# Attention in float32 on one core: groups of six key tiles with two half tiles copied out of PSUM by VectorE, an earlier load of the first queries, and warm-up products spread out

## The chip, the core and the metric

The kernel runs on one core of a Trainium2 chip. The metric is device time in microseconds of one execution. A core has five engines that run side by side and meet at semaphores: TensorE (PE in the profile, its weight loads PEld), VectorE (DVE), ScalarE (ACT), GpSimd (POOL) and SyncE (SP), which here issues most DMAs. Matrix products are written to PSUM[...]; all else lives in SBUF.

## What is computed

The reference is a chain of four layers on an image of 48 channels and 128 x 128 pixels, each with a group normalisation ahead and a residual sum behind it. The change touches layer 0 alone, which is attention over all 16384 pixels:

```
x = x + _L0_conv_ref(_gn(x), qkv_w, dw_w, proj_w, temperature)
...
qkv = jnp.einsum('bchw,oc->bohw', x, qkv_w)
qkv = conv_general_dilated(qkv, dw_w, ..., feature_group_count=3 * c)
q, k, v = jnp.split(qkv, 3, axis=1)
q = _l2norm(q)
k = _l2norm(k)
attn = softmax(einsum('bnc,bmc->bnm', q, k) * temperature)
out = einsum('bnm,bmc->bnc', attn, v)
return einsum('bchw,oc->bohw', out, proj_w)
```

Layers 1 to 3 (sweeps of 1-d convolutions, a patch convolution, a scan) follow and are the same in both kernels.

## The kernel before

**Conv.** `attention` loads the image in four pieces (SP, L139), computes the statistics of the normalisation (L237 and `group_stats`, L72 to L88) and makes queries, keys and values band by band: eight bands of 16 rows, two steps each. The 1x1 and the depthwise convolution are folded into weights `wt`, and the projection is folded into the values' part of them by four transposes and four products at the start (`pt`). Then 12 products that nobody reads (`keep_running`, tile `p`) run on TensorE ahead of the statistics' products (L74, L83). Normalised queries are written to DRAM (`qm`), each as a high and a low part, and are read back per chunk by `moving(c)`, eight DMAs on SP's queue (L174) into a tile `m`. Keys stay in SBUF as three parts (`kh`, `kl` and a joined rest, `x`). After the last band the first queries are loaded; then a branch on the temperature leads to `attend`.

**Attention.** `attend` loops over 32 chunks of 512 queries. The 64 key tiles of a chunk (each has 128 keys of the first half of the image and 128 of the second) go in groups of G = 5: twelve groups of five and one of four. Per tile, `scores` runs three products for each of the two halves on 64 rows of TensorE (the halves side by side) into two PSUM banks `s`, out of a pool of seven; ScalarE turns each half into `e` by an exponential (SBUF, G + 3 = 8 buffers of two halves). After the scores of a group, TensorE adds up the group before it: `sums` multiplies `e` with the values and their column of ones into the eighth bank, `acc`, the two halves in its upper and lower 64 partitions. So TensorE's order is: scores of group g, sums of group g-1, scores of group g+1, and so on.

**End of a chunk.** Its last group is summed behind the scores of group 0 of the next chunk. `Finish` then copies `acc` to `both` (ScalarE). After group 1, `divide` brings the lower half down (`second`, ScalarE), adds the halves (`y`, VectorE, L505), takes the reciprocal (VectorE, L508) and sends it to the other partitions by three DMAs (`recs`). After group 2, `result` multiplies, adds the residual and takes statistics on VectorE (L515 to L517).

**Order.** Products and ScalarE's instructions in these stages keep the order of the source (`InOrder`, whose line is L49 for all of them). VectorE, GpSimd and SP have no such wrapper: the framework's scheduler sets their order, and waits between engines are on tiles and on buffers of pools that are reused.

```
es = [(j, scores(m, j)) for j in range(g * G, min((g + 1) * G, KT))]
...
for i, e in behind:
    sums(acc, i, e)
if c and g == 0:
    finish = Finish(c - 1, acc)
if c and g == 1:
    finish.divide()
if c and g == 2:
    finish.result()
```

Of the kernel before, what the change touches and what calls it, by code (L numbers as in the profile page):

```python
# [19 lines left out]
F32 = mybir.dt.float32  # L20
F16 = mybir.dt.float16
F32R = mybir.dt.float32r
AF = mybir.ActivationFunctionType
# [4 lines left out]
C = 48  # L28
H = W = 128
N = H * W  # L30
CH = 512
# [65 lines left out]
def keep_running(pe, out, lhsT, rhs, n):  # L97

    for _ in range(n):
        pe.matmul(out, lhsT=lhsT, rhs=rhs, start=True, stop=True)  # L100
# [21 lines left out]
def attention(ctx, tc, x1, mp, const, ins):  # L122
# [3 lines left out]
    nc = tc.nc  # L126
    ident, blk = const["ident"], const["blk"]
    NQ = N // CH
    HALF = N // 2
    PART = 2048  # L130

    images = ctx.enter_context(tc.tile_pool(name="l0_x", bufs=1))
    image = []
    for i in range(HALF // PART):
        t = images.tile([128, PART], F32, name=f"x{i}")
        nc.gpsimd.memset(t[32:64], 0.0)
        for half in range(2):
            at = half * HALF + i * PART
# [20 lines left out]
    absT = kv.tile([128, 1], F32, name="absT")  # L159
    nc.vector.tensor_mul(absT, temp, sgn)  # L160

    def moving(c):

        m = mp.tile([128, 2, CH], F32R, name="m")
        high, low = qm[0:C, c * CH : (c + 1) * CH], qm[C:, c * CH : (c + 1) * CH]
        for half in range(2):
            at = 64 * half
            for i, to, x in (
                (0, 0, high),
                (0, C, low[C:]),  # L170
                (1, 0, low[0:32]),
                (1, 32, low[0:32]),
            ):
                nc.sync.dma_start(m[at + to : at + to + x.shape[0], i].bitcast(F32), x)  # L174
        return m
# [19 lines left out]
    with ExitStack() as a:  # L195
        act, pe = InOrder(tc, nc.scalar), InOrder(tc, nc.tensor)
# [4 lines left out]
        ps = a.enter_context(tc.tile_pool(name="l0_aps", bufs=4, space=PSUM))  # L201
# [5 lines left out]
        NB = H // R  # L207
# [4 lines left out]
        w1 = spare[:, 0 : 4 * 192].rearrange("c (t o) -> c t o", t=4)  # L212
        wt = packed_weights(nc, wp, "wt", ins["l0_w"], ins["l0_dw"], 192, w1)

        values = wt[:, :, 128:192]
        turned = spare[0:64, 4 * 192 : 4 * 192 + CH].rearrange("c (t o) -> c t o", t=4)
        pt = ps1.tile([128, 4, 2, 64], F32, name="pt").rearrange("c t n o -> c t (n o)")
        for t in range(4):
            pe.transpose(pt[0:64, t, :], values[:, t, :], ident)
        act.copy(turned, pt[0:64])  # L220
        pt = ps1.tile([128, 4, 2, 64], F32, name="pt")
        for t in range(4):
            pe.matmul(pt[:, t, 0, :], lhsT=turned[:, t, :], rhs=proj, start=True, stop=True)
        act.copy(values, pt[:, :, 0, :])

        K2 = 64 + C

        def piece(i):
            n, at = divmod(i * CH, PART)
            return image[n][:, at : at + CH]  # L230

        for i in range(NQ // 2 - 4):
            idle = ps.tile([128, CH], F32, name="p")
            keep_running(pe, idle, ident[0:K2], piece(i)[0:K2], 1)
        halves = wp.tile([K2, NQ // 2, 6], F32, name="halves")
        for i in range(NQ // 2):
            nc.vector.bn_stats(halves[:, i, :], piece(i)[0:K2])  # L237
        mean, rstd = group_stats(nc, wp, ps2, halves, const["gmat2"], name="pss")
# [154 lines left out]
            return scale, split, get  # L393

        cur = band(0)
        last = None
        for b in range(NB):
            nxt = band(b + 1) if b + 1 < NB else None
            for y in range(0, R, 8):
                p = [ps.tile([128, CH], F32, name="p") for _ in range(2)]  # L400
                pv = ps1.tile([128, CH], F32, name="pv")
                conv(p, pv, cur, y)
                more = take((b * R + y) * W, p, pv)
                if last:
                    last[1](act, last[2])
                last = more
            cur = nxt

    first = moving(0)
    small = nc.values_load(absT[0:1, 0:1].bitcast(mybir.dt.int32))
    bits = int(np.float32(32.0).view(np.int32))
    keys = kh, kl, rest_k
# [20 lines left out]
@with_exitstack  # L435
def attend(ctx, tc, keys, v, moving, m, x1, absT, const, ins, last):

    nc = tc.nc
    act, pe = InOrder(tc, nc.scalar), InOrder(tc, nc.tensor)
    ident, st = const["ident"], const["st"]
    NQ = N // CH
    KT = N // 2 // 128
    G = 5

    ep = ctx.enter_context(tc.tile_pool(name="l0_e", bufs=G + 3))
    sp = ctx.enter_context(tc.tile_pool(name="l0_b", bufs=1))  # L450
    ep2 = ctx.enter_context(tc.tile_pool(name="l0_add", bufs=1))
    ps_s = ctx.enter_context(tc.tile_pool(name="l0_ps", bufs=7, space=PSUM))
    ps_a = ctx.enter_context(tc.tile_pool(name="l0_pa", bufs=1, space=PSUM))


    sides = [slice(0, 64), slice(64, 128)]

    def scores(m, j):
        s = [ps_s.tile([128, CH], F32, name="s") for _ in sides]
        for n in range(3):  # L460
            k, at = key_tile(keys, n, j)
            for half, part in enumerate(sides):
                pe.matmul(
                    s[half],
                    lhsT=k[part, at],
                    rhs=m[part, n // 2],
                    start=(n == 0),
                    stop=(n == 2),
                )
        e = ep.tile([128, 2, CH], F32, name="e")  # L470
        for half in range(2):
            act.activation(e[:, half], s[half], AF.Exp, scale=absT)
        return e

    def sums(acc, j, e):

        for half, to in enumerate(sides):
            pe.matmul(
                acc[to],
                lhsT=v[:, half * KT + j, :],  # L480
                rhs=e[:, half, :],
                start=(j == 0),
                stop=(j == KT - 1),
            )

    def spare(name):

        return sp.tile([128, CH], F32, name=name)

    class Finish:  # L490


        def __init__(self, c, acc):
            self.c = c
            self.cols = slice(c * CH, (c + 1) * CH)
            self.xres = spare("xres")[0:C]
            nc.sync.dma_start(self.xres, ins["x"][:, self.cols])
            self.both = spare("both")
            act.copy(self.both, acc)

        def divide(self):
            second = spare("second")[0:64]
            act.copy(second, self.both[64:128])
            self.y = spare("y")[0:64]
            nc.vector.tensor_add(self.y, self.both[0:64], second)  # L505

            rec = spare("rec")[0:64]
            nc.vector.reciprocal(rec[32:64], self.y[32:64])  # L508
            self.rec = spare("recs")[0:C]
            for i in range(0, C, 64 - C):  # L510
                nc.sync.dma_start(self.rec[i : i + 64 - C], rec[C:64])

        def result(self):
            y = self.y[0:C]
            nc.vector.tensor_mul(y, y, self.rec)  # L515
            nc.vector.tensor_add(y, y, self.xres)
            nc.vector.bn_stats(st[:, self.c, :], y)  # L517
            nc.sync.dma_start(x1[:, self.cols], y)

    def end():  # L520

        cols = slice(N - CH, N)
        xres = spare("xres")[0:C]
        nc.sync.dma_start(xres, ins["x"][:, cols])
        o = spare("both")
        act.copy(o, acc)
        p = ps_s.tile([128, CH], F32, name="s")[0 : 64 + C]
        pe.matmul(p, lhsT=add, rhs=o, start=True, stop=True)
        rec = spare("rec")[0:C]
        nc.vector.reciprocal(rec, p[64 : 64 + C])  # L530
        nc.vector.tensor_mul(rec, p[0:C], rec)
        nc.vector.tensor_add(const["end"], rec, xres)
        nc.vector.bn_stats(st[:, NQ - 1, :], const["end"])

    names = {("f", 0): "xres", ("f", 1): "both", ("hl", 0): "second", ("hl", 1): "y"}
    own = {key: spare(name) for key, name in names.items()}

    def get(name, n):
        return own[name, n]

    scale, split = last
    scale(get)
    add = adder(nc, ep2, ident)
    behind, finish, acc, ahead = [], None, None, m
    for c in range(NQ):
        m = ahead
        for g in range(-(-KT // G)):
            es = [(j, scores(m, j)) for j in range(g * G, min((g + 1) * G, KT))]
            if g == 0 and c + 1 < NQ:
                ahead = moving(c + 1)  # L550
            if c == 0 and g == 2:
                split(act, get)
            for i, e in behind:
                if i == 0:
                    acc = ps_a.tile([128, CH], F32, name="acc")
                sums(acc, i, e)
            if c and g == 0:
                finish = Finish(c - 1, acc)
            if c and g == 1:
                finish.divide()  # L560
            if c and g == 2:
                finish.result()
            behind = es
    for i, e in behind:
        sums(acc, i, e)
    end()
# [1403 lines left out]
```

## Time and profile before

| What | Value |
|---|---|
| median of 3 runs | 7298.08 us (7297.69 to 7302.37) |
| profiled execution | 7313.33 us, span 7311.5 us |
| PE busy | 5935.4 us (81% of the span) |
| ACT busy | 4575.9 us (63%) |
| DVE busy | 3442.6 us (47%) |
| POOL busy | 2869.3 us (39%) |
| exponentials `e<-s` | 4096, mean 694 ns |
| products `acc<-e,v` | 8192 records, two per product, mean 597 ns |
| products `s<-m` | 3 x 4096, mean 389 to 421 ns |
| from the first score product to the last sum | 267.7 to 3677.3 us |

The page divides the span into 40 slices of 183 us; a digit is the busy share in tenths. The first slice and a half are the conv, then attention runs to about the twentieth slice, then come the other layers. An instruction's mean duration is longer than its share of the engine's time where instructions overlap: exponentials follow each other every 0.58 us, and the two halves of a score product run side by side.

### The profile page before, as it was taken

Reading aid. Unit: us, or ns where it says so; the run is one execution under the profiler, and the core shown is the slowest. Engines: PE = TensorE matmul, PEld = TensorE weight load, DVE = VectorE, ACT = ScalarE, POOL = GpSimd, SP = SyncE. Lnnn points to the kernel's source line nnn. Section 1 sums busy time; section 2 is a strip of 40 time slices with the busy share of each in tenths; the row PEclk is TensorE's granted clock in tenths of the full one; section 3 lists DMA queues with packets and bytes.
Section 4 is the critical chain, followed back from the end, with each engine's and each line's share of the span. In section 5 each row is a group of like instructions: output and inputs, shape, how many; then the busy total and the mean of one; then the engine's idle time right before and its main releaser. Section 6 shows DMA issues by size and latency. Waiting matters only on the chain.

```text
span 7311.5 us, 198657 instructions
## 1 busy us (share of the span) xinstructions
PE 5935.4 (81%) x89706; PEld 3563.8 (49%) x89706; DVE 3442.6 (47%) x3012; ACT 4575.9 (63%) x6826; POOL 2869.3 (39%) x655
## 2 busy tenths in 40 slices
PE   8899999999999999999999999455545545555555
PEld 3455555555555555555577755243433434444444
DVE  7400000000000000000044534799999999999998
ACT  3577777777777777777733023666676666666665
POOL 3200000000000000000010322699999999999998
PEclk9999999999999999999999999677767666666666
DMA  4200000000000000000010020565556666666775
GB/s 81 60 7 10 8 7 10 9 6 10 10 8 7 10 9 7 10 10 8 8 31 21 6 51 16 128 165 157 161 155 166 160 156 159 158 164 167 180 179 147
DMA packets 201818, 515.72 MB, mean 71 GB/s; under 512 B 41859, under 2 KB 73650, under 8 KB 199058
## 3 DMA queue, kind: packets, MB, share of 16 engines
q1 hardware_dynamic: 194135, 495.59, 26.4%
q8 instruction: 704, 11.53, 0.7%
q10 hardware_dynamic: 6827, 7.35, 0.4%
q14 instruction: 152, 1.25, 0.1%
HBM read 447.73 MB, written 29.36 MB: 65 GB/s over the span
## 4 chain that ended last, share of the span: by engine, by line
PE 58%; DVE 26%; issue 6%; POOL 4%; ACT 2%; DMA 2%; SPq 1%; ACTq 0%; DVEq 0%; POOLq 0%
PE acc L49 24%; DVE h L1722 22%; PE s L49 21%; PE p L49 7%; POOL h L1715 3%; PE y L49 2%; DMA du<-rep 1%; PE pc L49 1%; DVE xb L49 1%; PE pp L49 1%; PE po L49 1%; DVE rn L360 1%; ACT dA L49 1%; DVE y L49 0%; POOL y L1118 0%
## 5 line engine op out<-in xcount | busy, mean ns | idle before, releaser
L49 ACT ACTIVATE e<-s,absT 128x512 f32<-128x512 f32 x4096 | 2450.5, 694 | 884.2 <-PE s L49 741.7
L1715 POOL TENSOR_TENSOR h<-du,bt 128x3072 f32<-128x3072 f32 (+1 forms) x386 | 2559.2, 6667 | 94.7 <-DMA du<-rep 67.7
L1722 DVE TENSOR_TENSOR_SCAN h<-dA,carry,h 128x1024 f32<-128x1024 f32 x864 | 1940.0, 2325 | 40.6 <-ACT dA L49 27.0
L49 PE MATMUL acc<-e,v 128*64 128x512 f32 x8192 | 1849.4, 597 | 0.0
L49 ACT ACTIVATE dA<-dt,a 128x1024 f32<-128x1024 f32 x1152 | 1287.3, 1118 | 870.4 <-DVE h L1722 859.2
L49 PE MATMUL y<-h,cw 128*32 128x48 f32 x49152 | 900.0, 246 | 945.1 <-issue 503.7
L505 DVE TENSOR_TENSOR y<-both,second 64x512 f32<-64x512 f32 x31 | 21.2, 683 | 3021.6 <-ACT second L49 3021.6
L49 PEld LDWEIGHTS y<-h,cw 128*32 128x32 f32 x49152 | 810.0, 140 | 1073.2 <-issue 664.8
L789 POOL MEMSET xb<- 128x256 f32 (+1 forms) x2 | 0.7, 408 | 3383.3 <-ACT absT L420 3383.3
L49 PEld LDWEIGHTS acc<-e,v 128*64 128x64 f32 x8192 | 551.3, 137 | 1083.4 <-issue 1077.9
L49 PE MATMUL s<-m,kh 64*128 64x512 f32 x4096 | 956.0, 421 | 17.0 <-DMA m<-qm 16.5
L49 PE MATMUL s<-m,x 64*128 64x512 f32 x4096 | 914.6, 390 | 1.2 <-DMA m<-qm 1.1
L49 PE MATMUL s<-m,kl 64*128 64x512 f32 x4096 | 903.8, 389 | 0.0
L49 PEld LDWEIGHTS s<-m,kh 64*128 64x128 f32 x4096 | 473.1, 184 | 467.9 <-ACT e L49 289.6
L1722 DVE TENSOR_TENSOR_SCAN h<-dA,h 128x1024 f32<-128x1024 f32 x288 | 634.9, 2268 | 44.8 <-ACT dA L49 37.0
L49 PEld LDWEIGHTS s<-m,x 64*128 64x128 f32 x4096 | 477.7, 184 | 84.0 <-issue 6.7
L49 PEld LDWEIGHTS s<-m,kl 64*128 64x128 f32 x4096 | 448.1, 185 | 49.4
L49 PE MATMUL yz<-ev,sel 128*8 128x48 f32 x4096 | 192.7, 260 | 272.4 <-ACT ev L49 269.6
L49 PEld LDWEIGHTS yz<-ev,sel 128*8 128x8 f32 x4096 | 162.1, 106 | 328.2 <-ACT ev L49 299.5
L49 PE MATMUL p<-xb,l_w 112*48 112x78 f32 (+8 forms) x6096 | 226.4, 223 | 18.0 <-DVE xb L49 7.4
L49 PE MATMUL p<-xa,l_w 112*48 112x78 f32 (+8 forms) x6096 | 227.6, 224 | 14.9 <-DVE xa L49 5.9
L49 PEld LDWEIGHTS p<-xb,l_w 112*48 112x48 f32 x6096 | 193.0, 123 | 51.5 <-DVE xb L49 36.0
(221 smaller groups left out, 3752.5 us busy)
## 6 DMA issues: line engine op xcount, KB each, us to landing
du<-rep SPq DMA_DIRECT2D x768, 256.0 KB
dt<-rep SPq DMA_DIRECT2D x768, 256.0 KB
m<-qm SPq DMA_DIRECT2D x128, 64.0 KB
m<-qm SPq DMA_DIRECT2D x64, 96.0 KB
rep<-dd SPq DMA_DIRECT2D x24, 192.0 KB
yd<-ys ACTq DMA_DIRECT2D x256, 12.0 KB
qm<-hl SPq DMA_DIRECT2D x30, 128.0 KB
rest<-xa SPq DMA_DIRECT2D x90, 38.0 KB
```

Source lines behind the costliest of these rows:

```text
L49: ins = method(*args, **kwargs).ins
L360: nc.vector.reciprocal(rn, nrms[n])
L505: nc.vector.tensor_add(self.y, self.both[0:64], second)
L789: nc.gpsimd.memset(b[:, lines, pad], 0.0)
L1715: nc.gpsimd.tensor_mul(h[:, p, ks], du.unsqueeze(1).to_broadcast([128, ks.stop - ks.start, LC]), r["bt"][:, ks],)
L1722: nc.vector.tensor_tensor_scan(h[:, p, k, :], dA, h[:, p, k, :], carry[:, i, k : k + 1] if ci else 0.0, ALU.mult, ALU.add,)
```

## The change

Three edits.

1. In `attend`, G is 6, so that a chunk has ten groups of six and one of four, and `e` has G + 4 = 10 buffers. In groups of more than four tiles, VectorE copies the second half of the first and of the second tile from PSUM into the place in `e` where its result belongs. ScalarE takes the first halves of tiles 1, 2 and 3, then the two copied halves in place from SBUF, then the second half of tile 3 and the other tiles. `second` is copied by VectorE instead of ScalarE. In the source, `divide` and `result` stand directly behind the group's scores instead of behind the sums.
2. The first queries (`moving(0)`, eight DMAs) are loaded at the head of band 4 of 8 instead of after the last band.
3. The unread products are 11 instead of 12 and are spread: six ahead of the transposes, two between the transposes and the projection's products, three behind.

```
+        wake(0, 6)
         for t in range(4):
             pe.transpose(pt[0:64, t, :], values[:, t, :], ident)
         act.copy(turned, pt[0:64])
+        wake(6, 8)
...
         act.copy(values, pt[:, :, 0, :])
-        for i in range(NQ // 2 - 4):
-            idle = ps.tile([128, CH], F32, name="p")
-            keep_running(pe, idle, ident[0:K2], piece(i)[0:K2], 1)
+        wake(8, 11)
...
         for b in range(NB):
+            if b == NB // 2:
+                first = moving(0)
...
-    first = moving(0)
...
-    G = 5
-    ep = ctx.enter_context(tc.tile_pool(name="l0_e", bufs=G + 3))
+    G = 6
+    ep = ctx.enter_context(tc.tile_pool(name="l0_e", bufs=G + 4))
...
+        def exp(e, half, s):
+            act.activation(e[:, half], s, AF.Exp, scale=absT)
+        for n, j in enumerate(js):
+            s, e = scores(m, j)
+            if len(js) > 4 and n < 2:
+                exp(e, 0, s[0])
+                nc.vector.tensor_copy(e[:, 1], s[1])
+                waiting.append(e)
+            else:
+                exp(e, 0, s[0])
+                while waiting:
+                    t = waiting.pop(0)
+                    exp(t, 1, t[:, 1])
+                exp(e, 1, s[1])
...
         def divide(self):
             second = spare("second")[0:64]
-            act.copy(second, self.both[64:128])
+            nc.vector.tensor_copy(second, self.both[64:128])
...
-            es = [(j, scores(m, j)) for j in range(g * G, min((g + 1) * G, KT))]
+            es = group(m, range(g * G, min((g + 1) * G, KT)))
+            if c and g == 1:
+                finish.divide()
+            if c and g == 2:
+                finish.result()
...
-            if c and g == 1:
-                finish.divide()
-            if c and g == 2:
-                finish.result()
```

More of the change, by code (lines that the diff above doesn't have):

```diff
@@ L213, in attention, with piece, wake @@
         wt = packed_weights(nc, wp, "wt", ins["l0_w"], ins["l0_dw"], 192, w1)
+        K2 = 64 + C
+        def piece(i):
+            n, at = divmod(i * CH, PART)
+            return image[n][:, at : at + CH]
+        def wake(first, end):
+            for i in range(first, end):
+                idle = ps.tile([128, CH], F32, name="p")
+                keep_running(pe, idle, ident[0:K2], piece(i)[0:K2], 1)
+        wake(0, 6)
         values = wt[:, :, 128:192]
@@ L224, in attention @@
         act.copy(values, pt[:, :, 0, :])
[L226 to L230, printed above, removed]
-        for i in range(NQ // 2 - 4):
-            idle = ps.tile([128, CH], F32, name="p")
-            keep_running(pe, idle, ident[0:K2], piece(i)[0:K2], 1)
+        wake(8, 11)
         halves = wp.tile([K2, NQ // 2, 6], F32, name="halves")
@@ L395, in attention @@
         cur = band(0)
-        last = None
+        last = first = None
         for b in range(NB):
+            if b == NB // 2:
+                first = moving(0)
             nxt = band(b + 1) if b + 1 < NB else None
@@ L469, in scores, with group @@
                 )
[L470 to L473, printed above, removed]
+        return s, ep.tile([128, 2, CH], F32, name="e")
+    def group(m, js):
+        waiting, es = [], []
+        def exp(e, half, s):
[12 more added lines that the diff above has]
+                exp(e, 1, s[1])
+            es.append((j, e))
+        return es
     def sums(acc, j, e):
```

## The prediction

> **What bounds the kernel now.** I read the page's engine shares by slice first, then the chain that ended last, then the waits and the order in time of a few groups of the attention stage, and last the granted clock around idle stretches. The change touches attention alone, and the first two views say that this stage is TensorE's.
>
> ```profile
> PE   8899999999999999999999999455545545555555
> PEclk9999999999999999999999999677767666666666
> PE acc L49 24%; DVE h L1722 22%; PE s L49 21%; PE p L49 7%; POOL h L1715 3%; PE y L49 2%; DMA du<-rep 1%; PE pc L49 1%; DVE xb L49 1%; PE pp L49 1%; PE po L49 1%; DVE rn L360 1%; ACT dA L49 1%; DVE y L49 0%; POOL y L1118 0%
> ```
>
> The scores (s) and the sums (acc) hold 45% of the chain. By their first and last product they run from 267.7 to 3677.3 us: 3410 us for 32 chunks, 106.5 each. VectorE stands still there (it waits 97 us per chunk for `second`). Here is one group of five tiles in order of time (start, duration):
>
> ```profile
> 2003.32 0.50 PE L49 MATMUL s<-m,kh 64*128 64x512 f32 x2
> ...
> 2004.38 3.57 ACT L49 ACTIVATE e<-s,absT 128x512 f32<-128x512 f32 x6 [1.90 <-PE s L49]
> ...
> 2006.17 0.60 PE L49 MATMUL s<-m,kh 64*128 64x512 f32 x2
> ...
> 2007.17 4.51 PE L49 MATMUL acc<-e,v 128*64 128x512 f32 x20
> ...
> 2008.36 2.42 ACT L49 ACTIVATE e<-s,absT 128x512 f32<-128x512 f32 x4 [0.40 <-PE acc L49]
> ...
> 2011.61 0.50 PE L49 MATMUL s<-m,kh 64*128 64x512 f32 x2
> ```
>
> Scores take 3.85 us and sums 4.44, so a group is 8.29. The same view gives 2.95 for the scores of four tiles and 3.58 for the sums of four. From the start-to-start steps, a tile costs 3 x 0.2275 = 0.68 of scores and 0.86 of sums, and each group 0.22 + 0.16 for the two turns. Five tiles should then score in 3.63; the other 0.21 is the last tile's wait (0.60 instead of 0.39 per pair): with seven score banks its second half needs the bank of the third exponential. ScalarE is not the bound: 10 x 0.576 per group ((3.57 - 0.694)/5 apart).
>
> [...]
>
> [...] L516 and L517 follow 0.03 us after L515's 3.33 us wait for a DMA, though they depend on it. [...]
>
> [...]
>
> ```profile
> 4602.90:4606.31 3.41, 3.41 (x10) 1.50 (x9) 1.39 (x3) 3.38 (x4) 0.00 (x0) 1.00 0.00 0
> 4606.31:4609.72 3.41, 1.00 (x3) 0.17 (x1) 2.41 (x3) 3.38 (x4) 0.00 (x0) 1.00 0.00 0
> 4609.72:4613.13 3.41, 1.73 (x2) 0.84 (x3) 3.41 (x4) 2.63 (x5) 0.00 (x0) 0.50 0.00 0
> 4613.13:4616.55 3.42, 3.42 (x5) 1.35 (x4) 2.62 (x4) 3.23 (x4) 0.00 (x0) 0.50 0.00 0
> 4616.55:4619.96 3.41, 3.41 (x9) 1.52 (x8) 1.44 (x3) 3.38 (x5) 0.00 (x0) 1.00 0.00 0
> ```
>
> The columns are the stretch, its length, busy time of PE, PEld, DVE, ACT, POOL, granted clock, DMA. The clock changes only every 3.41 us. A window that is busy for 1.00 of 3.41 us is enough for half clock in the next, and a well-filled one brings full clock back. Counted over all full-clock windows of this trace: busy under 40%, 145 of 145 are followed by half clock; 40 to 60%, 29 of 100; above, none of 1366. I go by these counts.
>
> **The change, part by part.**
>
> *Groups of six with two copies.* A chunk's 64 tiles become ten groups of six and one of four (11, not 13). VectorE's copies free the banks of tile 1's and 2's second half; ScalarE then takes the three first halves, the two copied halves, and the rest. Counted from the group's first score, exponentials start at 1.06, 1.74, 2.43; the copies end at about 1.8 and 2.5 (0.69 each: nearest row, a 128x512 copy out of PSUM). The sixth tile wants banks at 3.52 and has them, so the 0.21 wait goes. Per chunk: 12 x 0.21 = 2.5, and two groups' turns 2 x 0.38 = 0.8. ScalarE needs 12 x 0.6 = 7.2 of 9.6 us, and ten e buffers, four free, hold it up no longer. The copies cost TensorE nothing while VectorE is idle. With `second` off ScalarE 0.2 goes (scores of 4.12 in the third group against 3.85, -0.05 in the second), and 0.2 of wait for m after the chunk's last group, which is now covered by 5.30 instead of 4.44 of sums. Sum: **-3.7 per chunk**.
>
> *Where VectorE is not idle.* The rows of a chunk's end:
>
> ```profile
> 2085.61 0.59 ACT L49 COPY both<-acc 128x512 f32<-128x512 f32 x1 [1.08 <-PE acc L49]
> ...
> 2093.61 0.68 DVE L505 TENSOR_TENSOR y<-both,second 64x512 f32<-64x512 f32 x1 [97.75 <-ACT second L49]
> ...
> 2094.33 3.34 DVE L508 RECIPROCAL rec<-y 32x512 f32<-32x512 f32 x1
> ```
>
> The source issues the division after group 1's copies, but the built program orders VectorE in each later chunk: `second`, `y`, group 1's first copy, **the reciprocal**, group 1's second copy. From group 0's first score: its scores 4.32 and the sums of four tiles 3.58, so group 1 starts at 7.90. ScalarE's last exponential starts at 2.43 + 9 x 0.576 = 7.61, `both` ends at 8.19 + 0.59 = 8.78. VectorE: `second` (not in this trace; between 0.37, in line with 0.34 for 48x512 as a quarter of L94's 1.34, and 0.69; I take 0.4) to 9.2, y to 9.9, first copy to 10.6, reciprocal to 14.0, second copy to 14.7 (15.1 at the upper end). The sixth tile of group 1 wants that bank at 7.90 + 0.11 + 5 x 0.68 = 11.4. Everything behind it on TensorE waits: **+3.3 to 3.7, I take 3.4, in 31 chunks**. ScalarE waits too, with nine exponentials left, 5.2 us, hidden under 5.3 of sums. The products that wait for `recs` are done before group 2's copies.
>
> *What that idle time does to the clock.* 3.1 to 3.4 us idle on windows of 3.41 leaves one window under 45% busy in most phases (about 8 in 10). The half-clock window after it costs up to 1.7, and a partly filled one keeps the clock down once more. Ends: 0 and 3.3; I take **+1.9**.
>
> *First queries in mid conv.* Eight DMA issues (3.6 us of SP's queue) move ahead of a band's loads; SP has room there (some 17 us of issues in a band's 25). After conv, TensorE's 13.66 us wait for m goes, but late next is VectorE: scale, the adder and the second reciprocal run to 271.4, and the first copy stands behind them, so the fifth tile starts near 272, where ScalarE's first exponential ran before. With chunk 0's own 3.7 I take -4.8 (0 to -10).
>
> *Products mixed.* Group statistics' product L74 came at 36.44, behind 12 warm-up products, though its input was ready at 31.7. Eleven, six of them ahead of the transposes, should end near 27: -4.6 (0 to -5).
>
> **Sum.** 31 x (-3.7 + 3.4 + 1.9) = +49; -4.8 - 4.6 gives +40. The profiled execution took 7313.33 us (span 7311.5), 0.2% over the median of 7298.08; I lay the difference on the median: 7338, rounded to **7337**.
>
> **Rivals.**
> - *The clock holds.* 31 x -0.3 - 9.4 = -19: 7279, faster. For it: the idle stretch is a little under a window, and full clock survives half-idle windows in 71 of 100. Against: the 145 of 145. This is the other side: it decides at a cold cost under about 0.6 per chunk.
> - *No stall*: the reciprocal does not hold the copy, or another bank is free. 31 x -3.7 - 9.4 = -124: 7174. Against: seven banks, and 97 us idle does not help an engine that is late only in group 1.
> - *Cold twice*: stall 3.8 and 3.3 of half clock: 31 x 3.4 - 9 = +96: 7394.
> - *The copies do not do what they should* (late in every group): a wait of 0.6 in each six-tile group takes back 6 per chunk, over 7500.
>
> **How the numbers follow.** Forecast 0.58, clock holds 0.23, no stall 0.07, cold twice 0.09, copies late 0.03. Under 0.2% (14.6 us) this kernel's measurement tells nothing from no change. Slower 0.58 + 0.09 + 0.03 = 0.70, less 0.01 of the forecast's low edge; of the clock's rival 0.12 falls within 0.2% and 0.11 below; so faster 0.18, same 0.13, slower 0.69. The range leaves out no stall, copies late, and part of cold twice: 7268 to 7390. The forecast's own is 7310 to 7375.
>
> **What would show it.** Right: scores of group 1 at some 7.7 us in 31 chunks, with PE waiting for the VectorE copy; six-tile groups of 9.6 elsewhere; half clock in short windows once per chunk; L74 near 32; first scores near 258 but the fifth tile near 272. Wrong: a copy ahead of the reciprocal, clock 1.00 from 400 to 3600, or other groups above 9.7.

## The result and the profile after

The changed kernel takes **7376.15 us** (median of 4 runs, 7366.34 to 7379.88); before it was 7298.96 us (4 runs, 7297.69 to 7302.37). The ratio is 1.0103, with a 95% interval from 1.0085 to 1.012: about 75 us slower (62 to 88). The forecast of 7337 had the sign and the mechanism, and about half of the size. The time lies just past the upper end of the forecast's own range (7310 to 7375).

The profiled execution of the changed kernel took 7366.34 us (span 7364.5), 53 us more than the profiled one of before. First the page's rows for TensorE, its clock, and the chain that ended last:

```profile
PE   8999999999999999999999999455545545554555
...
PEclk9999999999999999999999989677766767776667
...
PE acc L49 24%; DVE h L1749 21%; PE s L49 18%; PE p L49 6%; POOL h L1742 3%; PE y L49 2%; ACT e L49 2%; DVE rec L535 1%; DMA du<-rep 1%; PE pc L49 1%; DVE xb L49 1%; PE po L49 1%; DVE rn L367 1%; ACT dA L49 1%; PE pp L49 1%
```

At this resolution the first two rows look as before. The new entry in the chain is `DVE rec L535`: the reciprocal of the softmax division, which was not in this chain before, now lies on the path that sets the end, together with ScalarE's `e`. In order of time, groups 1 and 2 of a chunk show how (start, duration; group 1's scores begin at 2110.88):

```profile
2111.79 0.42 DVE L530 COPY second<-both 64x512 f32<-64x512 f32 x1 [6.37 <-ACT both L49]
...
2112.24 0.69 DVE L532 TENSOR_TENSOR y<-both,second 64x512 f32<-64x512 f32 x1
...
2112.86 0.68 DVE L491 COPY e<-s 128x512 f32<-128x512 f32 x1
...
2113.56 3.34 DVE L535 RECIPROCAL rec<-y 32x512 f32<-32x512 f32 x1
...
2114.43 0.39 PE L49 MATMUL s<-m,kh 64*128 64x512 f32 x1
2116.94 0.69 DVE L491 COPY e<-s 128x512 f32<-128x512 f32 x1
...
2117.68 0.50 PE L49 MATMUL s<-m,kh 64*128 64x512 f32 x1 [2.86 <-DVE e L491]
...
2118.57 7.07 PE L49 MATMUL acc<-e,v 128*64 128x512 f32 x24
...
2125.57 0.50 PE L49 MATMUL s<-m,kh 64*128 64x512 f32 x2
...
2129.89 5.37 PE L49 MATMUL acc<-e,v 128*64 128x512 f32 x24
...
2135.20 0.50 PE L49 MATMUL s<-m,kh 64*128 64x512 f32 x2
```

VectorE's order is the predicted one: `second`, y, first copy, reciprocal, second copy. The second copy starts at 2116.94, when the reciprocal is done (2116.9); half of the sixth tile starts on time at 2114.43, the other half, whose bank that copy frees, comes 3.25 us later. Then the sums take 7.00 us (2118.57 to 2125.57) instead of the 5.31 of the next group (2129.89 to 2135.20). Those 1.7 us are a lower clock, which the same stretch shows in windows of 3.41 us (busy time of PE, PEld, DVE, ACT, POOL, then the granted clock, DMA share and GB/s):

```profile
2112.38:2115.79 3.41, 2.44 (x21) 1.64 (x17) 3.38 (x3) 2.23 (x4) 0.00 (x0) 1.00 0.00 0
2115.79:2119.21 3.42, 1.53 (x9) 0.82 (x11) 1.81 (x2) 1.55 (x3) 0.00 (x0) 1.00 0.08 19
2119.21:2122.62 3.41, 3.41 (x12) 0.97 (x8) 2.05 (x3) 2.97 (x6) 0.00 (x0) 0.50 0.11 28
2122.62:2126.03 3.41, 3.41 (x18) 1.14 (x16) 0.00 (x0) 0.44 (x1) 0.00 (x0) 1.00 0.18 44
```

The wait falls on two windows. The second is busy for 1.53 of 3.42 us (45%), and the next runs at half clock, with TensorE fully busy in it.

This chunk is one of the milder ones. In most chunks the wait ends within the half-clock window, so that this window is only partly busy. In the attention from chunk 1 on, the 22 half-clock windows that were busy for 68 to 77% were all followed by a second one at half clock, and the 27 that were busy throughout all by full clock. Here is such a chunk, whose group 1 starts at 1242.85:

```profile
1245.39:1248.81 3.42, 1.43 (x13) 0.71 (x9) 3.39 (x2) 1.18 (x2) 0.00 (x0) 1.00 0.00 0
1248.81:1252.22 3.41, 2.48 (x7) 1.13 (x9) 0.84 (x2) 2.45 (x4) 0.00 (x0) 0.50 0.12 29
1252.22:1255.63 3.41, 3.41 (x10) 0.95 (x8) 2.05 (x3) 1.80 (x3) 0.00 (x0) 0.50 0.21 58
1255.63:1259.05 3.42, 3.42 (x18) 1.15 (x16) 0.00 (x0) 0.74 (x2) 0.00 (x0) 1.00 0.00 0
```

By segments, over all chunks but the first (the score and sum products of the trace, from start to start; means, with the lowest and the highest in brackets):

| Per chunk, us | before | after |
|---|---|---|
| a chunk, mean of chunks 1 to 30 | 106.39 | 108.70 |
| scores of a full group | 3.85 (5 tiles) | 4.35 (6 tiles) |
| scores of group 1 | 3.84 | 8.26 (7.60 to 8.47) |
| sums behind them | 4.44 | 7.05 (5.30 to 7.49) |
| sums of other full groups | 4.44 | 5.30 |

Part of the longer scores is the wait and part is the clock. Where the clock stays full, the sums start 0.94 us after the end of the second copy. Reckoned from that copy's end in each chunk, group 1's scores would take 7.76 at full clock, so the wait is **3.41 us** (3.26 to 3.51). The rest, 8.26 - 7.76 = 0.50 in the scores and 7.05 - 5.30 = 1.75 in the sums, is the clock: **2.25 us**. It is uneven: 22 of the 31 chunks have two windows at half clock and lose 2.8 us, five have one and lose 1.7, and four lose nothing. Without wait and clock a chunk would take 108.70 - 3.41 - 2.25 = 103.04, so six-tile groups do gain 3.3 to 3.4.

Ahead of the attention stage, the place where TensorE, ScalarE and VectorE meet:

```profile
256.61 1.28 ACT L49 ACT_TABLE_LOAD   x1 [4.86 <-DMA qm<-hl]
...
258.65 0.79 PE L49 MATMUL s<-m,kh 64*128 64x512 f32 x1 [4.07 <-ACT e L49]
...
264.62 1.39 PE L49 MATMUL s<-m,kh 64*128 64x512 f32 x2 [3.05 <-DVE e L491]
```

The first score now starts at 249.98 us and no longer waits for its queries. But the table load ahead of ScalarE's first exponential waits 4.86 us for a write of `qm` out of SBUF, and TensorE, out of banks, waits 4.07 us for ScalarE. The first copies start at 263.88, behind VectorE's second reciprocal, and the fifth tile (264.62) waits for one of them. Chunk 0 takes 113.4 us instead of 108.2.

### The profile page after: what moved, and what is told of

Read it like the earlier page. It is cut to its first block, busy times and chain, and to the rows that moved or that the text cites. A ratio compares the mean times of both kernels' runs of the same rounds, so it can differ in the third digit from the quotient of the medians.

```text
span 7364.5 us, 199876 instructions
## 1 busy us (share of the span) xinstructions
PE 5900.5 (80%) x89704; PEld 3524.6 (48%) x89704; DVE 3895.8 (53%) x3683; ACT 4609.3 (63%) x6795; POOL 2870.4 (39%) x655
## 4 chain that ended last, share of the span: by engine, by line
PE 54%; DVE 27%; issue 7%; POOL 5%; ACT 4%; DMA 2%; SPq 0%; ACTq 0%; DVEq 0%; POOLq 0%
PE acc L49 24%; DVE h L1749 21%; PE s L49 18%; PE p L49 6%; POOL h L1742 3%; PE y L49 2%; ACT e L49 2%; DVE rec L535 1%; DMA du<-rep 1%; PE pc L49 1%; DVE xb L49 1%; PE po L49 1%; DVE rn L367 1%; ACT dA L49 1%; PE pp L49 1%
## 5 line engine op out<-in xcount | busy, mean ns | idle before, releaser
L49 ACT ACTIVATE e<-s,absT 128x512 f32<-128x512 f32 x3456 | 2144.1, 696 | 847.4 <-PE s L49 801.8
L491 DVE COPY e<-s 128x512 f32<-128x512 f32 x640 | 441.9, 691 | 2519.3 <-PE s L49 2499.3
L49 PE MATMUL s<-m,kh 64*128 64x512 f32 x4096 | 878.4, 412 | 100.4 <-DVE e L491 92.8
L49 PE MATMUL s<-m,kl 64*128 64x512 f32 x4096 | 840.0, 395 | 0.0
L49 PE MATMUL s<-m,x 64*128 64x512 f32 x4096 | 827.9, 390 | 0.2
L49 PEld LDWEIGHTS s<-m,kh 64*128 64x128 f32 x4096 | 399.9, 185 | 478.6 <-issue 261.7
L49 ACT ACTIVATE e<-e,absT 128x512 f32<-128x512 f32 x640 | 426.9, 712 | 101.5 <-DVE e L491 101.5
L49 PEld LDWEIGHTS s<-m,x 64*128 64x128 f32 x4096 | 407.8, 187 | 88.7 <-DMA m<-qm 0.6
L49 PEld LDWEIGHTS s<-m,kl 64*128 64x128 f32 x4096 | 400.8, 186 | 64.1
L49 PE MATMUL p<-xa,l_w 112*48 112x78 f32 (+7 forms) x6096 | 227.5, 223 | 14.9 <-DVE xa L49 5.9
```

Of the source, the lines that this page charges most:

```text
L49: ins = method(*args, **kwargs).ins
L491: nc.vector.tensor_copy(e[:, 1], s[1])
```

## The experiments

There are eight kernels. Each ratio is to the kernel before, run beside it on the same chip, which took 7308.69 us beside the first four and 7307.6 beside the others; so ratios, not times, are compared with the result above. A chunk is the mean of chunks 1 to 30 throughout.

### Put VectorE in the order of the source

The changed kernel, with the copies, the division and the result on VectorE wrapped as ScalarE's work already is, so that both copies of a group come ahead of the division:

```
+    vec = InOrder(tc, nc.vector)
...
-                nc.vector.tensor_copy(e[:, 1], s[1])
+                vec.tensor_copy(e[:, 1], s[1])
...
-            nc.vector.tensor_copy(second, self.both[64:128])
+            vec.tensor_copy(second, self.both[64:128])
...
-            nc.vector.reciprocal(rec[32:64], self.y[32:64])
+            vec.reciprocal(rec[32:64], self.y[32:64])
```

(`y` and the three steps of `result` are wrapped in the same way.)

> The changed kernel with VectorE's instructions of the attention stage held in the source's order, so that both copies of group 1 come ahead of second, y and the reciprocal; nothing is left out. My theory (the reciprocal between the two copies makes TensorE wait 3.3 us per chunk, and the clock loses some 2.4 to 2.9 us behind it): both go, 31 x 5.7 to 6.2 us, so 7376 becomes about 7190 (7180 to 7205), group 1's scores take 4.35 us as in the other groups, and the granted clock is 1.00 through the stage. Rival (groups of six are slow by themselves, since the copies come late [...]): group 1 mends, other groups stay, and the time stays above 7298.

Measured: 7190.22 us, ratio **0.9836** (0.9819 to 0.9852). Group 1's scores take 4.31, the sums behind them 5.30, a chunk 103.08. VectorE in groups 1 and 2 of a chunk:

```profile
2126.88 1.38 DVE L49 COPY e<-s 128x512 f32<-128x512 f32 x2 [6.55 <-PE s L49]
2128.29 0.42 DVE L49 COPY second<-both 64x512 f32<-64x512 f32 x1
2128.75 0.68 DVE L49 TENSOR_TENSOR y<-both,second 64x512 f32<-64x512 f32 x1
2129.47 3.34 DVE L49 RECIPROCAL rec<-y 32x512 f32<-32x512 f32 x1
2136.43 1.39 DVE L49 COPY e<-s 128x512 f32<-128x512 f32 x2 [3.62 <-PE s L49]
```

The same instructions at the same durations; only the two copies stand together ahead of the reciprocal. The reciprocal ends at 2132.8, and VectorE then stands idle for 3.6 us until group 2's copies are wanted. So the whole loss of the change is in this order. This kernel beats both: 1.6% under before.

### Halve what the copy waits for

As above, but the order is `second`, y, first copy, the reciprocal's first 256 columns, second copy, the other 256:

```
+        def first(self):
+            vec.reciprocal(self.inv[32:64, 0:256], self.y[32:64, 0:256])
+        def then(self):
+            vec.reciprocal(self.inv[32:64, 256:], self.y[32:64, 256:])
...
+                between = finish.first, finish.then
```

(each is called behind one of group 1's copies.)

> The changed kernel with VectorE's order as it was built there, but the reciprocal in two halves of 256 columns, the second behind group 1's second copy; nothing is left out. TensorE's wait shrinks from 3.3 to about 1.65 us, less than half of a clock window of 3.41 us. My theory (the clock falls only where a window is under about 45% busy): the clock stays at 1.00, the cost is the wait alone, 31 x 1.65 = 51 us over the kernel without the wait: about 7243 (7230 to 7255). Rival (what is lost behind the wait grows with the idle time): half of the wait and half of the clock's loss remain, about 7283.

Measured: 7250.82 us, ratio 0.9922 (0.9906 to 0.9939). Group 1's scores take 6.15 (so it waits 1.8), the sums behind them 5.30 in every chunk, a chunk 104.8. With half of the reciprocal (1.74 us) between the copies, 1.6 of the 3.4 us of wait go, and all of the clock's loss.

### Keep TensorE busy in the wait

The changed kernel, with unread products into the empty `acc` bank ahead of group 1's sixth tile. They are there for the clock alone:

```
+            if fill is not None and n == 5:
+                keep_running(pe, fill, ident, still, 7)
...
+            if c and g == 1:
+                acc = fill = ps_a.tile([128, CH], F32, name="acc")
```

> The changed kernel with seven products that nobody reads (identity by a piece of the values, written to the acc bank that the sums then start afresh) on TensorE in group 1 between the fifth and the sixth tile's scores, 3.0 us of work inside the wait; nothing is left out. VectorE's order and the wait stay. My theory (idle time alone brings the clock down): the clock stays at 1.00, group 1 takes as long as the wait, the sums of group 0 take 5.30 us again, about 7190 + 31 x 3.4 = 7296 (7285 to 7308). Rival (the slow sums behind the wait come from something else, such as the exponentials that ScalarE has left): the time stays at 7376 or rises.

Measured: 7396.26 us, ratio 1.0121 (1.0104 to 1.0138): a miss. The seven unread products take 6.2 us, 0.886 each, and outlast the wait by some 3 us: a chunk takes 109.45. What the run tells is that the clock is 1.00 from 400 to 3600 us and the sums are back at 5.30. Hence a second one with 3 products in place of 7 (3 x 0.886 = 2.7):

> As the run with seven unread products in group 1, but with three, since one took 0.86 to 0.89 us there (two passes) and not 0.43 as I had reckoned, so that seven filled 6.2 us and outlasted the wait by 2.9; nothing is left out. Three are 2.6 us inside a wait of 3.3. My theory (idle time alone brings the clock down): the clock stays at 1.00, group 1 takes as long as the wait with VectorE's order as in the changed kernel, the sums behind it 5.30 us: about 7190 + 31 x 3.5 = 7298 (7288 to 7310). Rival (the sums behind a long wait are slow for another reason): about 7190 + 31 x 5.2 = 7350 or more.

Measured: 7303.16 us, ratio **0.999** (0.9982 to 0.9999); a chunk takes 106.42. The same stretch of both kernels, of the changed one first (columns as in the windows above):

```profile
1000.00:2000.00 1000.00, 973.75 (x5888) 492.82 (x5886) 184.54 (x238) 724.03 (x1185) 0.00 (x0) 0.97 0.03 9
```

and with three unread products:

```profile
1000.00:2000.00 1000.00, 1000.00 (x6064) 504.50 (x6062) 194.12 (x248) 737.20 (x1211) 0.00 (x0) 1.00 0.03 9
```

The copy is still late by the same reciprocal, TensorE computes nothing more that is used, and yet more work passes through (1211 ACT instructions in the 1000 us, not 1185): 108.70 - 106.42 = 2.3 us per chunk were the clock's, as by the segments.

### Leave the copies out

The changed kernel with `if False:` in place of the condition of the copies; ScalarE takes both halves of each tile in turn.

> The changed kernel without VectorE's copies: groups of six, ScalarE takes all halves from PSUM in order; nothing is left out. My theory (without the copies the sixth tile waits for the fourth and fifth exponential): scores of every six-tile group take some 4.9 us instead of 4.35, ten times per chunk, but group 1 has no wait for VectorE and the clock stays at 1.00: about 7190 + 32 x 6 = 7380 (7340 to 7410). Rival (the copies bring nothing): 7190 to 7220.

Measured: 7400.33 us, ratio 1.0126 (1.0109 to 1.0143), a chunk 109.63. The last three tiles of an ordinary group (one row for each tile's first product):

```profile
2041.02 0.40 PE L49 MATMUL s<-m,kh 64*128 64x512 f32 x2
...
2041.70 0.59 PE L49 MATMUL s<-m,kh 64*128 64x512 f32 x2
...
2042.38 1.07 PE L49 MATMUL s<-m,kh 64*128 64x512 f32 x2
```

The durations grow from 0.40 to 1.07 as the pair of products waits for banks: a group's scores take 5.00 instead of 4.35, 0.65 in every group and no loss of clock. So the copies do their work in all groups but group 1. Without them a group of six is worse than one of five.

### Groups of five with the copies

The in-order kernel with G = 5 and 9 `e` buffers, to part the gain of the copies from that of longer groups:

```
-    G = 6
+    G = 5
-    ep = ctx.enter_context(tc.tile_pool(name="l0_e", bufs=G + 4))
+    ep = ctx.enter_context(tc.tile_pool(name="l0_e", bufs=9))
```

> As the run with VectorE in the source's order (7190 us), but with groups of five and nine e buffers; the two copies per group stay; nothing is left out. My theory (the copies remove the last tile's 0.2 us wait in each group, and six tiles instead of five save two groups' turns of 0.38 per chunk): scores of a group of five 3.66 us instead of 3.85, 32 x 0.8 = 26 us more than 7190: about 7216 (7205 to 7230). Rival (the gain is all in the larger group): near the kernel before less 12 us for the other two parts, about 7287.

Measured: 7222.37 us, ratio 0.9877 (0.9862 to 0.9893). Five tiles score in 3.62 to 3.63, where they took 3.85: the 0.21 wait of the prediction's reckoning is what the copies take away, and the longer group adds its turns (0.9836 against 0.9877).

### The mixed products alone

The kernel before with the third part of the change only (`wake(0, 6)`, `wake(6, 8)`, `wake(8, 11)`).

> The kernel before with the third part of the change alone: 11 unread products in three places instead of 12 in one; nothing is left out. My theory: the first product of the statistics comes at about 30 us instead of 36.4, and all later work with it: 5 to 8 us less. Rival (conv is held by its own engines or DMAs, and the lead is lost by its end): no change.

Measured: 7303.3 us, ratio 0.9997 (0.9989 to 1.0006): no change that can be measured, and a miss. The rows of the weights' multiplication and of the statistics' product show why; first the kernel before as it was profiled for the forecast:

```profile
18.46 0.96 DVE L114 TENSOR_TENSOR wt<-wt,band 128x768 f32<-128x768 f32 x1 [10.17 <-DMA wt<-in_l_dw_dram]
...
36.44 0.27 PE L74 MATMUL pss<-gn_mv,gmat 112*112 112x1 f32 x2
```

and the kernel with mixed products:

```profile
14.70 0.96 DVE L114 TENSOR_TENSOR wt<-wt,band 128x768 f32<-128x768 f32 x1 [6.76 <-DMA wt<-in_l_dw_dram]
...
30.84 0.36 PE L74 MATMUL pss<-gn_mv,gmat 112*112 112x1 f32 x2 [4.44 <-DVE gn_mv L72]
```

It looks like 5.6 us saved. But in that one execution of before the weights' DMA had landed 3.8 us late (18.46 against 14.70), and the transposes and the unread products behind them with it. In the next run, which keeps the old order of products, the weights' row comes at 14.63 and L74 at 31.20. The statistics (L72) are not ready sooner (30.20 with mixed products, 30.12 in the next run), so mixing is worth 31.20 - 30.84 = 0.4 us where the weights land in time. The times alone would still allow some 8 us in favour of the mixed products; it is these rows that speak against more than 0.4.

### The early queries alone

The kernel before with the second part only (`first = moving(0)` at the head of band 4).

> The kernel before with the second part of the change alone: the first queries are loaded at band 4; nothing is left out. My theory: TensorE's first score comes 10 us earlier, but ScalarE's first exponential only about 6, since it waits for the DMA of the last band's queries whose SBUF the e buffers take over: 4 to 7 us less. Rival (VectorE's scaling behind the branch holds the first groups anyway, or the eight loads delay a band): no change or slower.

Measured: 7292.7 us, ratio 0.9978 (0.9967 to 0.9988): 16 us (9 to 24) saved, more than expected. The traces show the lower part of this: attention ends at 3661.25 here and at 3670.95 in the kernel with mixed products alone, whose conv was not late either. Here is the row that the changed kernel has at 256.61:

```profile
252.85 1.28 ACT L49 ACT_TABLE_LOAD   x1
```

ScalarE goes on at once and chunk 0 takes 106.92. It waits for no write of `qm`, and in this kernel no copy stands in VectorE's queue. In the changed one chunk 0 takes 113.4: part of what the early queries bring is lost again. A part of this is VectorE's queue: the first six tiles' scores take 22.68 us in the changed kernel and 18.81 in the one without copies.

## Why the prediction was right in kind and short in size

**Groups of six with two copies: right.** Predicted -3.7 per chunk, measured -3.3 to -3.4 (103.04 by the segments and 103.08 with VectorE in order, against 106.39). The term that is off is the score step: six tiles take 4.35, where 4.32 was reckoned, and four 2.99 instead of 2.95. Over ten groups and one these make most of the 0.3 to 0.4 that are missing. That the copies are needed is shown by the kernel without them (5.00 instead of 4.35), and that they cost TensorE nothing where VectorE is idle by the kernel in order (4.31 to 4.35 in groups 1 and up).

**VectorE's order in group 1: right.** Predicted a wait of 3.4 in 31 chunks, measured 3.41. The reckoned end of the second copy, 14.7 - 7.9 = 6.8 us after group 1's first score, is where it lies (6.66 to 6.91). The forecast took it that the second copy would not pass the reciprocal on VectorE, and the trace shows that it did not: tile 2's products are done at 2112.53, a microsecond before the reciprocal starts (0.94 to 1.19 over the 31 chunks), and in every chunk the second copy starts within 0.04 us of the reciprocal's end. The runs that change only this order or the length of the reciprocal move the time by about the amount that it gives.

**The clock: right in kind, too small.** Predicted +1.9 per chunk (0 to 3.3), measured 2.25 by the segments and 2.3 by the run with three unread products. The prediction took the phase of the wait against the windows as free, and gave 8 in 10 a half-clock window. It was 27 of 31, and 22 of them lost a second window, which the prediction had named but charged little for. The phase is not free: 21 of chunks 1 to 30 took 109.2 to 109.3 us, which is 32 windows of 3.413, so the next chunk meets the windows in the same, bad phase. In the clock's record of the stage the 22 half-clock spells of two windows are 6.83 us long and the five of one 3.41, and 22 stretches of full clock between them are 102.4 us each, 30 windows. The nine other chunks took 106.4 to 108.6. That the half clock itself sets this period is argued from these lengths; what is shown is that with three unread products, where the clock stays full, all of these chunks take 106.4 to 106.5.

The counts by which the forecast went hold for the changed kernel as a whole: of its full-clock windows busy under 40%, 141 of 141 were followed by half clock, at 40 to 60% 47 of 142, above that 1 of 1308. But they mix stages. In the attention from chunk 1 on, 22 of 23 windows that were busy for 40 to 48% were followed by half clock and none of 3 at 48 to 60%, while in the rest of the kernel it was 25 of 116. So the 29 in 100 of the prediction, which came nearly all from other stages, were too kind to this one; why a like share of busy time counts for less there is not shown. TensorE's idle time itself was never longer than 2.91 us in these chunks; the 27 windows ahead of the half-clock spells were busy for 15 to 47% of their 3.41 us, none of them idle throughout.

**First queries in mid conv: right in the sum, with the predicted successor.** The conv ended 7.6 us earlier in the changed trace than in that of before (the last `nrm` of ScalarE at 247.63 against 255.21; see the next point). With that taken off, the forecast's first scores near 258 come out at 257.6 and its fifth tile near 272 at 272.2 (it started at 264.62). The first score came 17.7 - 7.6 = 10.1 earlier, and chunk 0 took 5.2 longer: -4.9, where -4.8 was said. What the forecast did not see is that ScalarE's first exponential would wait for the write of `qm`, and that the early queries alone bring 9 us or more. The first did not decide here: the fifth tile waited for VectorE's copy, as was forecast.

**Products mixed: wrong.** Predicted -4.6, measured none that can be told, and 0.4 in the rows. The step that failed is the one from "L74 came at 36.44, behind 12 warm-up products" to a saving: it took one execution's start for the kernel's. That execution waited 10.17 us for the weights, as its row says, and took 7313.33 in all, 0.2% over the median. The prediction noted this and laid its own +40 on the median without asking where the 0.2% lay; a part of it lay in this start. The changed kernel's trace has L114 5.05 us earlier (13.41) and L74 6.6 earlier (29.87); the kernel with the old order of products has them 3.8 and 5.2 earlier, with the same 1.4 to 1.5 more at L74. So "L74 near 32" came true and is no evidence for the part.

**The sum.** Per chunk -3.35 + 3.41 + 2.25 = 2.31, times 31 is 72; with -4.9 for the start of attention and nothing for the mixed products it is +67, where the forecast had +40 (on 7298.08 that is 7338; the 7337 is a slip of one). The measured 75 lies between 62 and 88. Of the 27 us between the two sums 11 are the clock (31 x 0.35), 11 the gain (31 x 0.35) and 5 the mixed products. Beside the profiled execution of before it is 72 - 4.9 - 7.6 = 59; attention's end moved by 59.7 (3677.26 to 3736.96), and the layers behind it took 6.7 less in that one trace, which makes the 53 of the two executions.

**The rivals.** "The clock holds" is out: 0.97 in the stretch from 1000 to 2000 us, and the three unread products show what its holding would have given, 0.999 of before. "No stall" is the kernel in order: 0.9836 is 120 us, near its 124. "Cold twice" was wrong in its wait of 3.8 but right in that two windows in a row are at half clock, in 22 of 31 chunks, which lose 2.8 to the clock where it had 3.3. Its 7394 is nearer to the 7376 than the forecast's 7337 is; the chunks that lose less keep the mean between the two. "Copies late" is out, since groups other than group 1 stay at 4.35.

Left open: whether the executions that took 7373 to 7380 us differ from the profiled one (7366.34) by how long they stay in the rhythm of 109.2. If all chunks were in it, that would add 31 x 0.5 = 16 us. Their granted clock, 0.866 to 0.867 against 0.870, points that way, but the kernel before varies as much between its executions, and only one was profiled.

## What to carry to other kernels

When an idle engine is given a small job that another engine waits for, look at the built order on that engine for the longest instruction it can stand behind: here 0.69 us of copy behind 3.34 us of reciprocal, in one group of eleven, turned a gain of 1.6% into a loss of 1%. Keep both jobs in the order of need, or cut the long one: half of it left 1.8 of 3.4 us of wait and spared the clock. And read a saving off a start-up row only if a second execution shows the same row.

## What was not expected of the hardware

- The loop stayed in step with the clock's windows: 21 of 30 chunks took 109.2 to 109.3 us, 32 x 3.413, though the work and the wait without loss of clock are 106.4.
- The wait's cost was not proportional to its length: 1.8 us per chunk cost 1.8 (104.84 against 103.08), 3.4 us cost 5.6.
- The same share of busy time in a window did not mean the same for the next one: at 40 to 48% nearly all fell to half clock in the attention (22 of 23), at 40 to 60% in the other stages 25 of 116.
- Unread products within the wait gave 1.1% back (0.999 against 1.0103) where they ended before it did: three of them (128 columns by 512, float32) took 2.8 us. Seven took 6.2 us, and with them the kernel was slower than with none (1.0121).
